# Attention and feed-forward in one stream: a new order of products, statistics taken earlier, and rstd taken for several groups at once

## The chip, the cores and the metric

One core of one Trainium2 chip. The metric is the device time of one execution in microseconds (us), as the median of several executions. Executions fall into a fast state and a slower one (some 1.7% longer, 2877 us for the kernel before); verdicts here compare fast runs with fast runs. A profiled execution of each kernel gives the trace that the views below are taken from. Engines: PE = TensorE matmul, PEld = its weight load, DVE = VectorE, ACT = ScalarE, POOL = GpSimd.

## The reference

Three residual blocks, each with a layer norm in front: causal attention over 256 time steps, banded attention over 128 bands (distance up to 16), and a feed-forward of 128 to 512 to 128 with an exact gelu. All is in fp32.

```python
B, T, FB, C = (2, 256, 128, 128); heads = 4; BAND = 16; INNER = 512
def _ln(x, w, b, eps=1e-05):
    mu = x.mean(-1, keepdims=True)
    var = ((x - mu) ** 2).mean(-1, keepdims=True)
    return (x - mu) * jax.lax.rsqrt(var + eps) * w + b
...
xt = _ln(x, ln_t_w, ln_t_b).transpose(0, 2, 1, 3)
x = x + _mha(xt, ..., causal).transpose(0, 2, 1, 3)
xf = _ln(x, ln_f_w, ln_f_b)
x = x + _mha(xf, ..., band)
xn = _ln(x, ln_n_w, ln_n_b)
h = jax.nn.gelu(xn @ w1.T + b1, approximate=False)
... # x + h @ w2.T + b2
```

The part that matters most here is the `rsqrt` of the layer norm. The kernel calls its result rstd.

## The kernel before

Work comes in groups of 512 rows (four tiles of 128). There are 128 over-time groups (`OverTime`), then 16 runs of 8 band groups (`OverBands`) and 8 feed-forward groups (`FeedForward`). PE's products go by these names: `qp`, `kp`, `vp` (queries, keys, values), `sp` (scores), `rp` (row sums of the weights), `op` (weighted values), `yp` (output of the attention), and `hp` and `zp` (the two products of the feed-forward). ACT takes the exponentials (`pt`, `pf`) and the gelu (`hT`). DVE divides `op` by `rp` (`t`, `u`, `oT`), here by way of ACT's logarithm and exponential (`ln`, `r`). A "turned block" is the normalized group transposed: it goes out to `turned` and is fetched back as `xnT`, the operand of `qp`, `kp`, `vp` and `hp`.

The loop below emits instructions in a fixed order; in step n it emits pieces of groups n-2 to n+11, and every engine takes its own instructions in that order, one after the other. This last fact carries the whole case: a POOL instruction that waits holds up every POOL instruction emitted after it.

The layer norm of one group: mean and variance on DVE (`mv`), an addition and a power on POOL (`rstd`, 128x4: one element per tile and partition), the normalization on DVE (`xh`, four instructions).

```python
    def statistics(self):
        path, vector = self.path, self.path.vector
        self.mv = path.small.tile([P, NT, 2], F32, name="mv", bufs=16)
        stats = path.small.tile([P, NT, 6], F32, name="stats")
        for i in range(NT):
            vector.bn_stats(stats[:, i, :], self.src()[:, i, :])
        for i in range(NT):
            vector.bn_aggr(self.mv[:, i, :], stats[:, i, :])

    def root(self):
        path, gpsimd = self.path, self.path.gpsimd
        self.rstd = path.small.tile([P, NT], F32, name="rstd", bufs=16)
        gpsimd.tensor_scalar(self.rstd, self.mv[:, :, 1], EPS, None, ALU.add)
        gpsimd.tensor_tensor(self.rstd, self.rstd, path.k.mhalf, ALU.pow)

    def normalize(self):
        path, vector = self.path, self.path.vector
        self.xh = path.work.tile([P, NT, P], F32, name="xh", bufs=2)
        for i in range(NT):
            vector.tensor_scalar(
                self.xh[:, i, :], self.src()[:, i, :], self.mv[:, i, 0:1], self.rstd[:, i : i + 1],
                ALU.subtract, ALU.mult,
            )
```

Attention's bias add on POOL (a 128x512 addition, called `res<-x,orow` in the over-time stage and `x<-x,orow` for the bands; the feed-forward groups have one like it, `res<-x,rows_sb`):

```python
    def bias(self):
        self.path.gpsimd.tensor_tensor(
            self.dst(), self.src(), self.path.k.orow[self.which].unsqueeze(1).to_broadcast([P, NT, P]), ALU.add
        )
```

Masks, sums and the weighted values of the over-time groups. `mask(s)` is on POOL, the first half's sum is on POOL and the second half's on DVE; PE's `rp` (row sums of the weights) needs both halves:

```python
    def first_mask(self):
        self.mask(0)
        self.add(self.path.gpsimd, 0)

    def second_half(self):
        self.scores(1)

    def second_function(self):
        self.weights(1)

    def second_mask(self):
        self.mask(1)

    def last_sum(self):
        self.add(self.path.vector, 1)

    def weigh(self):
        path = self.path
        p, v, W = self.p, self.v, self.W
        rp = path.bank([P, 2, 2 * P], "rp")
        sums = p.rearrange("p s h (n q) -> p s h n q", q=P)[:, :, :, 0:4:3, :]
        for h in range(H):
            path.tensor.matmul(rp[rows_of(h), :, :], path.k.ones[:, 0:D], sums[:, :, h], start=True, stop=True)
        op = path.bank([P, 2, 2 * P], "op")
        for s in range(2):
            for h in range(H):
                r = rows_of(h)
                path.tensor.matmul(op[r, s, :], v[:, 2 * s, r], p[:, s, h, 0 : 2 * P], start=True, stop=False)
            for h in range(H):
                r = rows_of(h)
                path.tensor.matmul(
                    op[r, s, P : 2 * P], v[:, 2 * s + 1, r], p[:, s, h, 2 * P : W], start=False, stop=True
                )
        self.op = op.rearrange("p s q -> p (s q)")
        self.rp = rp.rearrange("p s q -> p (s q)")
```

The loop. `A` is 8. `feeds[i]` and `bands[i]` tell whether group n-2+i is of that kind.

```python
        for n in range(-11, len(groups) + 2):
            feeds = [at(n - 2 + i, FeedForward) for i in range(5)]
            bands = [at(n - 2 + i, OverBands) for i in range(5)]
            do(n + 11, "load")
            do_at(n + 4, OverTime, "statistics")
            if bands[2] and feeds[1]:
                self.scalar.preload_act_table_set(EXP_SET)
            do(n, "first_half", "first_function", "first_mask")
            do_at(n + 2, Attention, "fetch")
            do_at(n + 1, FeedForward, "fetch")
            do_at(n + 2, FeedForward, "normalize", "turn")
            do_at(n + 3, Attention, "normalize", "turn")
            do_at(n + 3, FeedForward, "statistics", "root")
            do_at(n + 4, OverTime, "root")
            if bands[2]:
                do(n, "second_mask")
            do(n - 1, "weigh")
            if not feeds[1]:
                do(n - 1, "invert")
            if bands[2]:
                do(n - 2, "output", "finish")
            do(n - 1, "divide")
            do(n, "second_half", "second_function")
            if not bands[2]:
                do(n, "second_mask", "bias")
                do_at(n + A, OverBands, "bias", "statistics", "root")
            do(n + 1, "queries_keys", "take_query", "take_key")
            if not bands[2]:
                do(n - 2, "output", "finish")
            do(n + 1, "values", "take_values")
            do(n, "last_sum")
```

Of the kernel before, what the change touches and what calls it, by code (L numbers as in the profile page):

```python
# [19 lines left out]
P = 128  # L20
# [18 lines left out]
def load_constants(ctx, tc, x, t_wiT, t_woT, f_wiT, f_woT, w1T, w2T, cols, rows):  # L39
# [24 lines left out]
    k.mhalf = const.tile([P, NT], F32, name="mhalf")  # L64
# [7 lines left out]
def shifted_path(tc, k, x, out):  # L72
# [5 lines left out]
    with ExitStack() as ctx:  # L78
# [36 lines left out]
        def norm_transposed(src, w_col, b_col):  # L115
# [8 lines left out]
            nc.gpsimd.tensor_tensor(rstd, rstd, k.mhalf, ALU.pow)  # L124
# [311 lines left out]
class Group:  # L436
# [6 lines left out]
    def __init__(self, path, src, dst, before=None, store=None):  # L443
        self.path, self.src, self.dst = path, src, dst
        self.before, self.store = before, store

# [8 lines left out]
    def statistics(self):  # L455
        path, vector = self.path, self.path.vector
        self.mv = path.small.tile([P, NT, 2], F32, name="mv", bufs=16)
        stats = path.small.tile([P, NT, 6], F32, name="stats")
        for i in range(NT):
            vector.bn_stats(stats[:, i, :], self.src()[:, i, :])  # L460
        for i in range(NT):
            vector.bn_aggr(self.mv[:, i, :], stats[:, i, :])

    def root(self):
        path, gpsimd = self.path, self.path.gpsimd
        self.rstd = path.small.tile([P, NT], F32, name="rstd", bufs=16)
        gpsimd.tensor_scalar(self.rstd, self.mv[:, :, 1], EPS, None, ALU.add)
        gpsimd.tensor_tensor(self.rstd, self.rstd, path.k.mhalf, ALU.pow)

    def normalize(self):  # L470
        path, vector = self.path, self.path.vector
        self.xh = path.work.tile([P, NT, P], F32, name="xh", bufs=2)
        for i in range(NT):
            vector.tensor_scalar(
                self.xh[:, i, :], self.src()[:, i, :], self.mv[:, i, 0:1], self.rstd[:, i : i + 1],
                ALU.subtract, ALU.mult,
            )
# [70 lines left out]
class Attention(Group):  # L548
# [45 lines left out]

    def divide(self):

        path, vector = self.path, self.path.vector
        t = path.work.tile([P, NT * P], F32, name="t", bufs=2)
        vector.tensor_tensor(by_rows(t), by_tile(self.rp), by_tile(self.r0), ALU.mult)
        u = path.work.tile([P, NT * P], F32, name="u", bufs=2)  # L600
        vector.tensor_tensor(by_rows(u), by_tile(self.op), by_tile(self.r0), ALU.mult)
        self.oT = path.work.tile([P, NT * P], F32, name="oT", bufs=2)
        vector.scalar_tensor_tensor(self.oT, t, 2.0, u, ALU.subtract, ALU.mult)
# [17 lines left out]
def product(path, out, weights, x):  # L621

    for c in range(P // D):
        path.tensor.matmul(out[rows_of(c)], weights[:, rows_of(c)], x, start=True, stop=True)


class OverTime(Attention):
# [65 lines left out]

    def weigh(self):
        path = self.path
        p, v, W = self.p, self.v, self.W
        rp = path.bank([P, 2, 2 * P], "rp")
        sums = p.rearrange("p s h (n q) -> p s h n q", q=P)[:, :, :, 0:4:3, :]
        for h in range(H):
            path.tensor.matmul(rp[rows_of(h), :, :], path.k.ones[:, 0:D], sums[:, :, h], start=True, stop=True)  # L700
        op = path.bank([P, 2, 2 * P], "op")
        for s in range(2):
            for h in range(H):
                r = rows_of(h)
                path.tensor.matmul(op[r, s, :], v[:, 2 * s, r], p[:, s, h, 0 : 2 * P], start=True, stop=False)
            for h in range(H):
                r = rows_of(h)
                path.tensor.matmul(
                    op[r, s, P : 2 * P], v[:, 2 * s + 1, r], p[:, s, h, 2 * P : W], start=False, stop=True
                )  # L710
# [59 lines left out]
class FeedForward(Group):  # L770

# [20 lines left out]
    def first_half(self):  # L792
        self.hp = {}
        self.hT = self.path.work.tile([P, self.path.k.NI, NT * P], F32, name="hT")
# [41 lines left out]
class BoundedPath:  # L836
# [38 lines left out]
    def groups(self, x, out):  # L875
# [3 lines left out]
        for b in range(B):  # L879
            for f0 in range(0, FB, GA):  # L880
# [22 lines left out]
                for g in range(NT):  # L903
                    yield OverTime(self, partial(part, "x", g), partial(part, "res", g), partial(load, g), partial(store, g))
        for b in range(B):
            for r0 in range(0, T, RUN):
                run = []
                for t0 in range(r0, r0 + RUN, GB):
# [25 lines left out]
                    run += [(g, part, load, store) for g in range(NT)]  # L934
                for i, (g, part, load, _) in enumerate(run):
                    group = OverBands(self, partial(part, "x", g), partial(part, "x2", g), partial(load, g))
                    if i == len(run) - 1:
                        group.by_vector = 2
                    yield group
                for g, part, _, store in run:  # L940
                    yield FeedForward(self, partial(part, "x2", g), partial(part, "res", g), None, partial(store, g))

    def run(self, x, out):
# [17 lines left out]
        for n in range(-11, len(groups) + 2):  # L961
            feeds = [at(n - 2 + i, FeedForward) for i in range(5)]
            bands = [at(n - 2 + i, OverBands) for i in range(5)]
            do(n + 11, "load")
            do_at(n + 4, OverTime, "statistics")
            if bands[2] and feeds[1]:
                self.scalar.preload_act_table_set(EXP_SET)
            do(n, "first_half", "first_function", "first_mask")
            do_at(n + 2, Attention, "fetch")
# [3 lines left out]
            do_at(n + 3, FeedForward, "statistics", "root")  # L973
            do_at(n + 4, OverTime, "root")
# [3 lines left out]
            if not feeds[1]:  # L978
                do(n - 1, "invert")
            if bands[2]:  # L980
                do(n - 2, "output", "finish")
            do(n - 1, "divide")
            do(n, "second_half", "second_function")
            if not bands[2]:
                do(n, "second_mask", "bias")
                do_at(n + A, OverBands, "bias", "statistics", "root")
            do(n + 1, "queries_keys", "take_query", "take_key")
            if not bands[2]:
# [72 lines left out]
```

## Time and profile before

| | before |
|---|---|
| median of 3 executions | 2832.48 us (2829.37 to 2876.43) |
| span of the profiled execution | 2826.2 us, PE busy 98% |
| over-time stage (first q product to last `rp` of the stage) | 1015.3 us, 7.82 us a step |
| one run of 8 band and 8 feed-forward groups (first `hp` to the next run's) | 110.06 us: 65.07 with feed-forward, 44.98 with bands |

The last two rows are read from the timeline of PE. They are the measure used for every kernel below, since the two stages turn out to have different causes. The list of PE's waits holds almost nothing in the runs (beside the waits of the start, its only other line above 1 us is `rp` behind DVE `pt`, told in the prediction); the columns are what waited, for whom, then us in total, number of times, and the longest:

```profile
PE hp L831 <- DMA xnT<-turned: 3.0, 6, 0.9
```

One more stretch of before is needed later: POOL in the feed-forward part, in the timeline (start, duration, engine, line, operation, and in brackets the idle time before it and what ended it).

```profile
1230.01 0.23 POOL L831 TENSOR_SCALAR rstd<-mv 128x4 f32<-128x4 f32 x1 [1.40 <-DVE mv L831]
1230.33 1.04 POOL L831 TENSOR_TENSOR rstd<-rstd,mhalf 128x4 f32<-128x4 f32 x1
1231.34 1.26 POOL L831 TENSOR_TENSOR res<-x,rows_sb 128x512 f32<-128x512 f32 x1
1232.05 2.37 DVE L831 TENSOR_SCALAR xh<-x,mv,rstd 128x128 f32<-128x128 f32 x4
1232.56 1.27 POOL L831 TENSOR_TENSOR x<-x,orow 128x512 f32<-128x512 f32 x1
```

Look at what starts POOL: it waits for DVE's `mv` of this step, does a power, and then two adds. Then come the band group's addition and power, and the next wait for statistics (1.15 us, at 1236.29). So no more than two bias adds come in a row in this stretch. (`xh` for a group takes 1.11 us when no add is near and 2.37 here.)

### The profile page before, as it was taken

To read this page: it belongs to the slowest core of one execution; us is meant where nothing else is said; L and a number is where in the kernel's file an instruction comes from. 1 tells how busy PE (TensorE), PEld (TensorE's weight loads), DVE (VectorE), ACT (ScalarE), POOL (GpSimd) and SP (SyncE) were. 2 spreads that over 40 slices of the span, in tenths; PEclk is the share of its full clock that TensorE was granted. 3 is DMA by queue.
4 is the path that set the end of the run, shared out by engine and by line. 5 is a ranking of instruction groups with operands and counts; after the bars stand their busy time and mean duration, and the time that the engine had idled before them with its cause. 6 is when DMAs were issued, how large, how long until landed. Compare 5 with 4: busy or idle time off the path is not lost.

```text
span 2826.2 us, 107020 instructions
## 1 busy us (share of the span) xinstructions
PE 2757.7 (98%) x44070; PEld 1858.9 (66%) x44070; DVE 2264.5 (80%) x6462; ACT 1865.2 (66%) x3408; POOL 2057.9 (73%) x2537
## 2 busy tenths in 40 slices
PE   5999999999999989999999999999999999999998
PEld 3666666666666656766766766666667667667666
DVE  5888888888888898788787787786887877877874
ACT  2777777777777767557557566566575575675664
POOL 3999999999999996676675676676666766656762
PEclk9999999999999999999999999999999999999999
DMA  5455545454554544534434434534435445344333
GB/s 122 126 148 133 140 129 146 131 140 130 147 140 129 135 126 123 144 105 106 128 106 120 129 102 122 131 94 130 115 101 141 106 107 130 102 121 114 87 95 84
DMA packets 471313, 343.90 MB, mean 122 GB/s; under 512 B 43296, under 2 KB 405152, under 8 KB 470816
## 3 DMA queue, kind: packets, MB, share of 16 engines
q1 hardware_dynamic: 469568, 335.92, 45.6%
q8 instruction: 349, 5.72, 0.8%
q14 instruction: 148, 1.21, 0.2%
q10 hardware_dynamic: 1248, 1.05, 0.1%
HBM read 169.03 MB, written 167.77 MB: 119 GB/s over the span
## 4 chain that ended last, share of the span: by engine, by line
PE 93%; DMA 2%; POOL 2%; DVE 2%; issue 0%; SPq 0%; ACT 0%; DVEq 0%; POOLq 0%
PE zp L831 16%; PE hp L831 16%; PE sp L831 13%; PE op L831 9%; PE rp L831 9%; PE qp L831 8%; PE yp L831 7%; PE vp L831 7%; PE kp L831 7%; DMA xnT<-turned 1%; DVE xh L831 1%; POOL pf L831 1%; POOL rstd L831 1%; DMA x<-in_x 1%; POOL pt L831 1%; DMA turned<-z 0%
## 5 line engine op out<-in xcount | busy, mean ns | idle before, releaser
L831 POOL TENSOR_SCALAR_AFFINE_SELECT pf<-pf 128x512 f32<-128x512 f32 x736 | 495.4, 688 | 273.1 <-ACT pf L831 248.0
L831 ACT ACTIVATE hT<-hp,b 128x512 f32<-128x512 f32 x512 | 345.2, 687 | 479.8 <-PE hp L831 470.3
L831 DVE TENSOR_SCALAR xh<-x,mv,rstd 128x128 f32<-128x128 f32 x1536 | 621.7, 465 | 15.4 <-POOL rstd L831 15.4
L831 PEld LDWEIGHTS zp<-w2T_sb,hT 128*128 128x128 f32 x4096 | 476.9, 192 | 56.1 <-issue 51.6
L831 ACT ACTIVATE pt<-sp 128x384 f32<-128x384 f32 x1024 | 419.6, 497 | 104.6 <-PE sp L831 104.6
L831 POOL TENSOR_TENSOR rstd<-rstd,mhalf 128x4 f32<-128x4 f32 x384 | 463.5, 1207 | 32.0
L831 PE MATMUL zp<-w2T_sb,hT 128*128 128x128 f32 x4096 | 480.4, 276 | 0.1
L831 PE MATMUL hp<-xnT,w1f 128*128 128x512 f32 x1024 | 474.8, 599 | 3.3 <-DMA xnT<-turned 3.0
L831 PE MATMUL sp<-qT,kT 32*128 32x128 f32 (+1 forms) x8192 | 398.3, 317 | 0.9 <-ACT kT L831 0.8
L831 POOL TENSOR_SCALAR_AFFINE_SELECT pt<-pt 128x512 f32<-128x512 f32 x512 | 315.3, 636 | 96.6 <-ACT pt L831 96.6
L831 PEld LDWEIGHTS sp<-qT,kT 32*128 32x128 f32 x8192 | 316.5, 186 | 85.8 <-issue 31.8
L831 DVE BATCH_NORM_STATS2 stats<-x 128x6 f32<-128x128 f32 x1536 | 326.8, 273 | 7.8 <-DMA x<-in_x 7.8
L831 POOL TENSOR_SCALAR rstd<-mv 128x4 f32<-128x4 f32 x384 | 94.9, 247 | 318.3 <-DVE mv L831 318.3
L831 ACT ACTIVATE pf<-sp 128x512 f32<-128x512 f32 x512 | 264.4, 603 | 62.5 <-PE sp L831 58.5
L831 PEld LDWEIGHTS hp<-xnT,w1f 128*128 128x128 f32 x1024 | 180.9, 190 | 176.9 <-issue 103.9
L831 PE MATMUL qp<-xnT,wf 128*32 128x512 f32 x2048 | 271.5, 602 | 26.1 <-DMA xnT<-turned 26.1
L831 PEld LDWEIGHTS yp<-wn,oT 128*32 128x32 f32 x8192 | 229.1, 110 | 99.6 <-issue 51.0
L831 DVE STREAM_TRANSPOSE z<-xh 128x512 f32<-128x512 f32 x384 | 273.2, 711 | 18.8 <-DMA turned<-z 5.6
L831 PEld LDWEIGHTS vp<-wf,xnT 128*32 128x32 f32 x8192 | 232.1, 110 | 78.2 <-issue 68.6
L831 DVE TENSOR_TENSOR pf<-pf,band 128x512 f32<-128x512 f32 x144 | 127.1, 892 | 188.8 <-ACT pf L831 181.3
L831 PE MATMUL yp<-wn,oT 128*32 128x128 f32 x8192 | 271.4, 273 | 0.0
L831 PE MATMUL vp<-wf,xnT 128*32 128x128 f32 x8192 | 270.6, 273 | 0.0
(87 smaller groups left out, 4029.4 us busy)
## 6 DMA issues: line engine op xcount, KB each, us to landing
turned<-z SPq DMA_DIRECT2D x1536, 64.0 KB, 2.0
xnT<-turned SPq DMA_DIRECT2D x384, 256.0 KB, 2.7
x<-in_x SPq DMA_DIRECT2D x128, 256.0 KB, 4.7
x<-res SPq DMA_DIRECT2D x256, 128.0 KB, 3.4
x<-x SPq DMA_DIRECT2D x128, 256.0 KB, 4.2
out<-res SPq DMA_DIRECT2D x256, 128.0 KB, 2.8
w1T_sb<-in_w1T ACTq DMA_DIRECT2D x1, 256.0 KB, 3.4
w2T_sb<-in_w2T ACTq DMA_DIRECT2D x1, 256.0 KB, 3.9
```

Of the source, the lines that this page charges most:

```text
L831: return self.tc.keep_in_program_order(emit(*args, **kwargs))
```

## The change

The intent: fewer instructions on POOL (a power for four groups at once in place of four powers), less switching of PE's tiling mode, and no waiting of `rp` for DVE.

1. **op before rp** in the over-time steps: half of `op`, then `rp`, then the other half.
2. **The change from bands to feed-forward** is emitted in another order (the flag `turn` of the loop), with an exact reciprocal on DVE for the last band group in place of ACT's ln and exp.
3. **Whole products** for q, k, v in the steps beside feed-forward groups, in place of four 32-column tiles.
4. **Statistics earlier**: feed-forward four steps ahead (was three), over-time eight ahead (was four).
5. **rstd for four groups at once** (two in the feed-forward): the `mv` of the batch lie in one tile, and the addition and power are emitted with the last group of the batch.

```diff
     def statistics(self):
-        path, vector = self.path, self.path.vector
-        self.mv = path.small.tile([P, NT, 2], F32, name="mv", bufs=16)
+        path, vector, n = self.path, self.path.vector, self.together
+        if self.slot == 0:
+            self.norm["mv"] = path.small.tile([P, n * NT, 2], F32, name="mv", bufs=4)
+        self.mv = self.norm["mv"][:, self.slot * NT : (self.slot + 1) * NT]
...
     def root(self):
-        path, gpsimd = self.path, self.path.gpsimd
-        self.rstd = path.small.tile([P, NT], F32, name="rstd", bufs=16)
-        gpsimd.tensor_scalar(self.rstd, self.mv[:, :, 1], EPS, None, ALU.add)
-        gpsimd.tensor_tensor(self.rstd, self.rstd, path.k.mhalf, ALU.pow)
+
+        path, gpsimd, n = self.path, self.path.gpsimd, self.together
+        if self.slot == n - 1:
+            rstd = path.small.tile([P, n * NT], F32, name="rstd", bufs=4)
+            gpsimd.tensor_scalar(rstd, self.norm["mv"][:, :, 1], EPS, None, ALU.add)
+            gpsimd.tensor_tensor(rstd, rstd, path.k.mhalf[:, 0 : n * NT], ALU.pow)
+            self.norm["rstd"] = rstd
...
+    def invert_exactly(self):
+        self.r0 = None
+        self.r = self.path.work.tile([P, NT * P], F32, name="ln", bufs=2)
+        self.path.vector.reciprocal(self.r, self.rp)
...
 def product(path, out, weights, x):
 
+    if not path.by_columns:
+        path.tensor.matmul(out, weights, x, start=True, stop=True)
+        return
...
     def weigh(self):
         path = self.path
-        p, v, W = self.p, self.v, self.W
+        op = path.bank([P, 2, 2 * P], "op")
         rp = path.bank([P, 2, 2 * P], "rp")
-        sums = p.rearrange("p s h (n q) -> p s h n q", q=P)[:, :, :, 0:4:3, :]
+        self.weigh_one(op, 0)
+        sums = self.p.rearrange("p s h (n q) -> p s h n q", q=P)[:, :, :, 0:4:3, :]
         for h in range(H):
             path.tensor.matmul(rp[rows_of(h), :, :], path.k.ones[:, 0:D], sums[:, :, h], start=True, stop=True)
...
+        self.weigh_one(op, 1)
...
+            turn = feeds[2] and bands[1]
+            self.by_columns = at(n - 1, Attention)
             do(n + 11, "load")
-            do_at(n + 4, OverTime, "statistics")
             if bands[2] and feeds[1]:
                 self.scalar.preload_act_table_set(EXP_SET)
             do(n, "first_half", "first_function", "first_mask")
+            if turn:
+                do(n, "second_half", "second_function")
             do_at(n + 2, Attention, "fetch")
             do_at(n + 1, FeedForward, "fetch")
             do_at(n + 2, FeedForward, "normalize", "turn")
             do_at(n + 3, Attention, "normalize", "turn")
-            do_at(n + 3, FeedForward, "statistics", "root")
-            do_at(n + 4, OverTime, "root")
+            do_at(n + 4, FeedForward, "statistics", "root")
+            do_at(n + A, OverTime, "statistics", "root")
             if bands[2]:
                 do(n, "second_mask")
             do(n - 1, "weigh")
-            if not feeds[1]:
-                do(n - 1, "invert")
-            if bands[2]:
+            do(n - 1, "invert_exactly" if turn else "invert")
+            if bands[2] or turn:
                 do(n - 2, "output", "finish")
             do(n - 1, "divide")
-            do(n, "second_half", "second_function")
+            if not turn:
+                do(n, "second_half", "second_function")
             if not bands[2]:
                 do(n, "second_mask", "bias")
-                do_at(n + A, OverBands, "bias", "statistics", "root")
+                do_at(n + A, OverBands, "bias")
+                if at(n - 1, FeedForward) and at(n - 2, OverBands):
+                    do_at(n + A - 1, OverBands, "statistics", "root")
+                if not turn:
+                    do_at(n + A, OverBands, "statistics", "root")
             do(n + 1, "queries_keys", "take_query", "take_key")
-            if not bands[2]:
+            if not bands[2] and not turn:
                 do(n - 2, "output", "finish")
```

Cut: the arguments that carry a batch's tiles to its groups, `normalize` reading its slice of the batch's rstd, the last band group of a run no longer masking two heads on DVE, and two buffers for `hT`.

## The prediction

> **What bounds the kernel now.** I read the page first (engine shares, chain, groups), then busy time in stretches, then the timeline and the chain of work inside one step of each stage. The page's first part and the head of its chain:
>
> ```profile
> span 2826.2 us, 107020 instructions
> PE 2757.7 (98%) x44070; PEld 1858.9 (66%) x44070; DVE 2264.5 (80%) x6462; ACT 1865.2 (66%) x3408; POOL 2057.9 (73%) x2537
> PE 93%; DMA 2%; POOL 2%; DVE 2%; issue 0%; SPq 0%; ACT 0%; DVEq 0%; POOLq 0%
> ```
>
> PE looks full: only 68.5 us of the span are not PE (2826.2 - 2757.7). The busy table by stretches places them: about 31 in the first 42 us, 5 up to 200 us, 8 between 1000 and 1080 us, 8 at the end, a few at transfers, and some 12 in 200 to 1000 us, which is 0.12 per step of 7.82 us. The program is 128 attention-over-time steps (to about 1055 us), then 16 runs of 8 band steps (6.43 us each) and 8 feed-forward steps (7.0 us each).
>
> That 0.12 is the interesting part. One over-time step, from the timeline of 608.9 to 618.9 us:
>
> ```profile
> 616.02 0.69 DVE L831 TENSOR_TENSOR res<-yp,res 128x512 f32<-128x512 f32 x1 [0.99 <-PE yp L831]
> 616.63 1.04 DVE L831 TENSOR_TENSOR pt<-pt 128x512 f32<-128x512 f32 x1
> 616.76 0.94 PE L831 MATMUL sp<-qT,kT 32*128 32x256 f32 x16
> 617.82 1.07 PE L831 MATMUL rp<-pt,ones 128*32 128x512 f32 x8
> ```
>
> DVE's pt sum ends at 616.63 + 1.04 = 617.67 and rp starts 0.15 later. Where the list of waits does name DVE pt as rp's releaser (8 times, 10.1 us), the distance is also 0.14 to 0.15. So in every over-time step rp waits shortly on DVE, below what the list shows. The step closes as a loop: yp (PE), res and pt (DVE), rp (PE). Without that wait sp would hand over at once, as the step's second sp does (starts 612.29, the next product at 613.16, 0.87 later; the first takes 617.82 - 616.76 = 1.06). The wait costs 0.19 us a step.
>
> At the change between bands and feed-forward the chain of work shows another cost, of PE itself:
>
> ```profile
> 1436.12 1.91 PE hp L831 x4
> 1438.04 1.08 PE rp L831 x8
> 1439.12 1.15 PE op L831 x31
> 1440.27 1.91 PE hp L831 x4
> 1442.18 1.01 PE yp L831 x32
> 1443.20 1.91 PE hp L831 x4
> 1445.11 3.59 PE zp L831 x32
> 1448.70 1.72 PE hp L831 x4
> 1450.42 1.01 PE yp L831 x32
> 1451.43 1.91 PE hp L831 x4
> ```
>
> hp (whole 128x128 weights) takes 1.72 behind another whole product and 1.91 behind one in four 32-column tiles; yp 0.87 inside a column stretch and 1.01 behind a whole one. Each excursion costs about 0.33 us.
>
> **What the Trainium skill says.** (1) "TensorEngine Tiling (Array Packing)", Tiling Modes, Key Properties: changing the tiling mode drains TensorE. The trace agrees: 1.91 against 1.72. (2) "SBUF — State Buffer", "SBUF: two separate sides": VectorE and GpSimd share a port pair, locked for the whole instruction when a VectorE instruction has two SBUF inputs or runs in a two-port mode. The trace agrees: the 128x512 oT took 0.69 us, and 1.77 beside a GpSimd add at 998 us. (3) "GPSIMD Engine Reference", section 3.1: about 2.6 cycles per element for a two-input op, done in a software loop. The 128x512 add at 1.28 us fits. For the power, no page has a figure. (4) "VectorE: DVE Perf Modes", the fixed hardware budget: reciprocal is an iterative divide with a repeat count of 8. From it I estimate 512 x 8 / 0.96 GHz = 4.3 us for one 128x512; the trace before has none.
>
> **Part 1: op before rp in the over-time steps.** weigh now does half of op, then rp, then the other half. Half an op is 1.30/2 = 0.65 us, so rp is asked for 0.65 later than before, and the wait of 0.19 goes. PE's work is the same. About 122 steady steps x 0.19 = 23 us; I count 21, for weight loads behind the mode switch.
>
> **Part 2: the change to feed-forward (16 times).** Before, the ten lines above last 1453.34 - 1436.12 = 17.2 us (16.9 where op does not wait, at 1215 us). After, the order of instructions has eight hp, rp, op, yp, four hp, zp, four hp, yp whole, four hp: 3.63 + 1.08 + 0.87 + 0.87 + 1.91 + 3.59 + 1.72 + 0.89 + 1.72 = 16.3. Saved 0.6 to 0.9, say 0.8 x 16 = 13 us.
>
> **Part 3: whole q, k, v products beside feed-forward (15 times, twice each).** qp 0.99 becomes 0.86 in each: 2 x 0.13 x 15 = 4 us.
>
> **Part 4: the end of the over-time stage.** From 991 to 1056 us the chain is POOL, then DVE: the band groups' bias (1.3 us) and rstd come on top, and for four steps statistics are taken twice. PE stands idle 7.9 us there, of which about 1.3 is Part 1's wait. With one set of statistics per step everywhere and three of four powers gone: -6 us, if the power of sixteen is short.
>
> **Part 5: the start.** PE starts its first product at 41.4 us, since the first turned block went out behind sixteen loads of x and the second turned block. Now four statistics and the fifth (1.1 us each) come before the first normalization, about 2.8 us later on DVE, but the loads still fill the queue to 33.3 us, and the first fetch is issued before the second turned block. Also op no longer waits for the pt sum at 54 us. I count -3 us.
>
> **Part 6: tables and the exact reciprocal.** Table loads fall from 80 to 32 (48 x 1.28 = 62 us of ACT), all beside PE work: the feed-forward stage has ACT idle 470 us for hp. The reciprocal puts up to 4.3 us on DVE, 16 times, in place of ACT's ln and exp and one DVE product. Its oT is wanted at about 1449.8 on the scale above, and comes at about 1445 + its duration: just in time. Counted 0.
>
> **Part 7: rstd.** GpSimd's additions and powers fall from 384 each to 128 each (32 + 32 of sixteen, 64 of eight):
>
> ```profile
> L831 POOL TENSOR_TENSOR rstd<-rstd,mhalf 128x4 f32<-128x4 f32 x384 | 463.5, 1207 | 32.0
> L831 POOL TENSOR_SCALAR rstd<-mv 128x4 f32<-128x4 f32 x384 | 94.9, 247 | 318.3 <-DVE mv L831 318.3
> ```
>
> This is off PE's path, as POOL has 0.67 us idle per step, so the saving is worth nothing directly. But the longer power stands in POOL's queue between the pt sum of one half and the mask of the other, which the pt sum of DVE and then rp wait for. In the step's timeline POOL gets there at 614.1; add 0.3 for the addition, up to 0.46 for the port (the power took 1.51 there against 1.037 free), the power P, half the masks 0.62, DVE's sum 1.0, release 0.15: 616.6 + P. rp is wanted at about 618.2 with op first. A power over about 1.6 us therefore stops PE, in 30 steps.
>
> Sum without such a stop: 21 + 13 + 4 + 6 + 3 = 47 us, from a fast level of about 2831: 2784.
>
> **Rivals.** (a) The power grows with its elements. 1.037 us for four, less the 0.22 of an addition, is 0.2 per element and 3.5 for sixteen: PE stops 1.9 us, 30 times, +57 us, and Part 4 turns to nothing: about 2847. For it: GpSimd works in a software loop, and 0.8 us of overhead on a power is hard to explain. Against: an author who batches will have seen batching pay. Weight 0.4. (b) The power has a large fixed part and grows a little, 1.8 to 2.2 us: some 10 us lost, about 2795. Weight 0.25. (c) Mostly fixed, up to 1.6 us: about 2784. Weight 0.35. (d) On top, the reciprocal comes too late for yp or delays the next normalizations: 1 us x 16 = +16. (e) DVE becomes the bound of the over-time step instead (6.7 of 7.63 us busy): unlikely, it keeps 0.9 us.
>
> **Range and chances.** The median of this mixture lies near 2794. The range takes (c) with a little more at one end and (a) at the other: 2770 to 2856. Faster by 2% needs under 2776, a saving of 56 us; all parts would have to come out at their best: 0.12. Slower by 2% is over 2889: rival (a) with (d) and more: 0.03. Within 2%: 0.85.
>
> **What would show it.** Over-time steps of 7.63 us and rp not at 0.15 behind DVE pt: Part 1 right. Steps of 7.82 still: Part 1 wrong. The row of rstd 128x16 decides the rivals: 1.6 us or less for (c); about 3.5, with rp idle every fourth step behind pt, for (a). hp at 1.91 twice rather than four times per run shows Part 2; yp waiting on oT shows (d). No idle PE at 1000 us shows Part 4, a first product before 41 us Part 5. The prediction would be wrong if the wait moves to another loop of the same length, or if the first op half behind the mode switch costs what the wait cost.

## The result

The changed kernel takes **3002.57 us** (3000.20 to 3004.66, four runs) against 2830.93 us beside it. The ratio of the fast runs is 1.0608 (95% interval 1.0590 to 1.0626): slower by 6%, and outside the predicted range. Ratios in this document are the mean time of one kernel's fast runs over that of the other's of the same rounds, so not quite the ratio of the medians. The result agrees with the reference, and so did every kernel below in the comparison that is run with each.

| | before | after | difference |
|---|---|---|---|
| over-time stage | 1015.3 us | 1081.3 us | +66.0 |
| one run | 110.06 us | 116.96 us | +6.90, times 16 = +110 |
| of it feed-forward part / band part | 65.07 / 44.98 | 70.63 / 46.34 | +5.56 / +1.36 |

The two stages give 176 us; the spans of the two profiles differ by 172.2. From the page of after, the engines' busy time and the chain of work by engine:

```profile
PE 2779.0 (93%) x42534; PEld 1855.0 (62%) x42534; DVE 2432.8 (81%) x6446; ACT 1801.7 (60%) x3328; POOL 1824.4 (61%) x2057
...
PE 56%; DVE 23%; POOL 9%; DMA 6%; issue 3%; ACT 2%; SPq 1%; DVEq 0%; POOLq 0%
```

POOL has 233 us less to do than before (1824.4 against 2057.9), just as intended, and the kernel is slower. PE has nearly the same work, but the chain that ends last, which was PE to 93%, is now PE to 56% only; DVE and POOL took the rest. PE's waits say where (the views of the changed kernels name another line, since all instructions are emitted by one helper line):

```profile
PE hp L858 <- DMA xnT<-turned: 55.9, 31, 3.8
PE yp L858 <- DVE t L858: 43.8, 32, 1.5
PE rp L858 <- DVE pt L858: 41.5, 33, 1.3
```

Two of these groups (`rp`, `yp`, about 32 each) belong to the over-time stage, which has 32 batches; `hp` belongs to the runs.

With its smaller lines the list has 84 us of waits in the runs, 5.3 us a run. The rest of what the runs lose is in waits too short for the list, and a part may be the clock: the trace's clock record has eleven stretches of 3.4 us at a granted clock of 0.50 in the runs of after and none in those of before. That is 1.7 us each at most, 19 us in all; the ten runs (of fifteen) that hold one took 117.2 us on average, the five others 116.5. What brings these stretches on was not tested; a_root4 and best_mix below, which lose nothing in the runs, have none there.

The groups of instructions concerned (times are busy us, then mean ns, then the idle time before them):

```profile
L858 POOL TENSOR_TENSOR rstd<-rstd,mhalf 128x16 f32<-128x16 f32 x64 | 200.1, 3127 | 5.3
L858 POOL TENSOR_TENSOR rstd<-rstd,mhalf 128x8 f32<-128x8 f32 x64 | 111.5, 1742 | 5.3
L858 DVE TENSOR_SCALAR xh<-x,mv,rstd 128x128 f32<-128x128 f32 x1536 | 753.9, 551 | 34.9 <-POOL rstd L858 34.9
```

The power costs by its elements: undisturbed it took 1.04 us for four, 1.67 for eight and 2.93 for sixteen, which is about 0.157 us an element and 0.41 fixed. DVE's normalizations took 753.9 us in all, against 621.7 before, with the same work.

**An over-time step with a batch**, from the timeline:

```profile
612.53 3.25 POOL L858 TENSOR_TENSOR rstd<-rstd,mhalf 128x16 f32<-128x16 f32 x1
...
615.75 1.22 POOL L858 TENSOR_SCALAR_AFFINE_SELECT pt<-pt 128x512 f32<-128x512 f32 x2
616.41 1.10 DVE L858 TENSOR_TENSOR pt<-pt 128x512 f32<-128x512 f32 x1 [1.78 <-POOL pt L858]
616.94 1.71 POOL L858 TENSOR_TENSOR res<-x,orow 128x512 f32<-128x512 f32 x1
617.44 3.72 DVE L858 TENSOR_SCALAR xh<-x,mv,rstd 128x128 f32<-128x128 f32 x4
617.66 1.06 PE L858 MATMUL rp<-pt,ones 128*32 128x512 f32 x8 [1.28 <-DVE pt L858]
...
623.57 1.08 PE L858 MATMUL yp<-wn,oT 128*32 128x128 f32 x32 [1.47 <-DVE t L858]
```

Read it as two blows from one power. First: the second mask stands behind the power, DVE's sum waits 1.78 us for it, and PE's `rp` waits 1.28. Second: POOL is now late, and does its backlog without a pause (add, masks, sum); DVE's `xh` lasts 3.72 us in place of 1.10. Taken singly, its four instructions end 0.08 to 0.09 us after one of POOL's each time (at 618.74, 619.32, 619.91 and 621.16), as it would be if the two engines take turns at the port pair of the prediction's point (2). DVE's `t` and `oT` stand behind it, and `yp` waits 1.47. The four steps from 600.94 to 634.62 last 33.68 us; four steps without a stall last 30.5.

**The feed-forward part of a run**, also from the timeline of after:

```profile
1658.84 0.24 POOL L858 TENSOR_SCALAR rstd<-mv 128x8 f32<-128x8 f32 x1 [10.11 <-DVE mv L858]
1659.16 1.67 POOL L858 TENSOR_TENSOR rstd<-rstd,mhalf 128x8 f32<-128x8 f32 x1
1660.79 1.27 POOL L858 TENSOR_TENSOR res<-x,rows_sb 128x512 f32<-128x512 f32 x1
1661.90 4.00 DVE L858 TENSOR_SCALAR xh<-x,mv,rstd 128x128 f32<-128x128 f32 x4
1662.03 1.34 POOL L858 TENSOR_TENSOR x<-x,orow 128x512 f32<-128x512 f32 x1
1663.33 1.27 POOL L858 TENSOR_TENSOR res<-x,rows_sb 128x512 f32<-128x512 f32 x1
1664.55 1.26 POOL L858 TENSOR_TENSOR x<-x,orow 128x512 f32<-128x512 f32 x1
1664.89 1.96 PE L858 MATMUL hp<-xnT,w1f 128*128 128x512 f32 x4 [0.66 <-DMA xnT<-turned]
```

This is the stretch to hold against the one shown of before. POOL waited 10.11 us for the statistics of a pair, while its bias adds stood behind that wait in its queue. Then four adds came in a row, where before there were two. Counted over the whole trace from 1180 us on, before never has more than two adds in a row; after has four in a row 15 times and eight in a row 15 times, so once each in a run. `xh` lasts 4.00 us: its last three instructions take 1.30 us each, and each ends 0.08 us after one of POOL's adds. The turned block of this group is fetched later, and PE's `hp` waits for the fetch (3.8 us at worst, 31 times in all).

### The profile page after: what moved, and what is told of

Its sections match the earlier page's. It is cut to its first block, busy times and chain, and to the rows that moved or that the text cites. A ratio compares the mean times of both kernels' runs of the same rounds, so it can differ in the third digit from the quotient of the medians.

```text
span 2998.4 us, 103522 instructions
## 1 busy us (share of the span) xinstructions
PE 2779.0 (93%) x42534; PEld 1855.0 (62%) x42534; DVE 2432.8 (81%) x6446; ACT 1801.7 (60%) x3328; POOL 1824.4 (61%) x2057
## 4 chain that ended last, share of the span: by engine, by line
PE 56%; DVE 23%; POOL 9%; DMA 6%; issue 3%; ACT 2%; SPq 1%; DVEq 0%; POOLq 0%
PE zp L858 10%; DVE xh L858 9%; PE hp L858 8%; PE sp L858 8%; PE op L858 5%; PE vp L858 5%; PE qp L858 5%; PE rp L858 5%; PE kp L858 4%; PE yp L858 4%; DVE stats L858 4%; POOL rstd L858 4%; DMA xnT<-turned 4%; POOL pt L858 2%; DVE z L858 2%
## 5 line engine op out<-in xcount | busy, mean ns | idle before, releaser
L858 DVE TENSOR_SCALAR xh<-x,mv,rstd 128x128 f32<-128x128 f32 x1536 | 753.9, 551 | 34.9 <-POOL rstd L858 34.9
L858 POOL TENSOR_SCALAR_AFFINE_SELECT pf<-pf 128x512 f32<-128x512 f32 x768 | 515.5, 687 | 279.1 <-ACT pf L858 252.8
L858 POOL TENSOR_SCALAR rstd<-mv 128x16 f32<-128x16 f32 (+1 forms) x128 | 32.8, 256 | 524.8 <-DVE mv L858 524.8
L858 POOL TENSOR_TENSOR rstd<-rstd,mhalf 128x16 f32<-128x16 f32 (+1 forms) x128 | 311.6, 2435 | 10.7
L858 PEld LDWEIGHTS yp<-wn,oT 128*32 128x32 f32 (+1 forms) x7808 | 230.5, 111 | 141.5 <-DVE t L858 73.6
L858 PE MATMUL yp<-wn,oT 128*32 128x128 f32 (+1 forms) x7808 | 272.6, 273 | 45.6 <-DVE t L858 43.8
L858 PE MATMUL qp<-xnT,wf 128*32 128x512 f32 (+1 forms) x1856 | 270.6, 600 | 28.8 <-DMA xnT<-turned 28.8
L858 PEld LDWEIGHTS vp<-wf,xnT 128*32 128x32 f32 (+1 forms) x7424 | 236.4, 113 | 75.8 <-issue 65.1
L858 ACT COPY v<-vp 128x512 f32<-128x512 f32 x256 | 150.2, 587 | 210.6 <-PE vp L858 210.6
L858 PE MATMUL vp<-wf,xnT 128*32 128x128 f32 (+1 forms) x7424 | 270.9, 273 | 1.5 <-DVE t L858 1.5
```

Of the source, the lines that this page charges most:

```text
L858: return self.tc.keep_in_program_order(emit(*args, **kwargs))
```

## The experiments

Twelve kernels were run, four at a time beside the kernel before on one chip. All profiled runs were in the fast state. "Stage" is the over-time stage and "run" one run, as in the tables above.

### Undo one part of the change, or do one part alone

**a_root4**: the changed kernel with rstd per group; everything else of the change stays.

```diff
-        if self.slot == n - 1:
-            rstd = path.small.tile([P, n * NT], F32, name="rstd", bufs=4)
-            gpsimd.tensor_scalar(rstd, self.norm["mv"][:, :, 1], EPS, None, ALU.add)
-            gpsimd.tensor_tensor(rstd, rstd, path.k.mhalf[:, 0 : n * NT], ALU.pow)
+        self.rstd = path.small.tile([P, NT], F32, name="rstd", bufs=16)
+        gpsimd.tensor_scalar(self.rstd, self.mv[:, :, 1], EPS, None, ALU.add)
+        gpsimd.tensor_tensor(self.rstd, self.rstd, path.k.mhalf[:, 0:NT], ALU.pow)
```

Cut: `statistics` and `normalize`, which go back to tiles per group in the same way.

> The changed kernel, but rstd taken for each group by itself again (384 powers of 128x4); everything else of the change stays. Theory 1 (the batch is the cause everywhere: a power of sixteen takes 2.9 us and holds POOL's queue, afterwards POOL runs its adds back to back and DVE's xh is locked out): over-time steps of 7.63 us each without a slow fourth, runs of bands and feed-forward back near 109 us, total about 2800. Theory 2 (the batch costs the over-time stage only, the reordered change to feed-forward with its reciprocal of 3.33 us on DVE costs the runs): over-time stage 97 us shorter than in the changed kernel, runs still about 116 us, total about 2905.

**a_noturn**: the changed kernel with part 2 undone (`turn = False`, the old places of the bands' statistics, two heads of the last band masked on DVE).

> The changed kernel with the old order at the change to feed-forward (second half of the hidden layer after the weighing, logarithm and exponential on ACT instead of the reciprocal, two heads of the last band masked on DVE); the batch of rstd stays. Theory 1: the runs stay slow, above 114 us each, total 2980 or more. Theory 2: runs near 110 us, total about 2900, and few waits of hp for xnT.

**b_oporder**: the kernel before with part 1 alone (the new `weigh`).

> The kernel before with only the order inside weigh of the over-time steps changed: half of op, then the sums rp, then the other half. If rp's hidden wait for DVE's pt sum (0.19 us per step) is what Part 1 says: steps of 7.63 us, total about 2808 (ratio 0.992). If the wait moves elsewhere: 7.82 and 2831.

**b_turn**: the kernel before with part 2 alone (order, exact reciprocal).

> The kernel before with only the new order at the change to feed-forward (four hidden products at once, the exact reciprocal on DVE, statistics of the next bands one step later there); two heads of the last band still masked on DVE, rstd per group. My prediction's Part 2: 13 us saved, total 2818. Theory 2: runs of 114 us or more, total 2890 or more, hp waiting for xnT in the second to fifth feed-forward group.

| | median us | ratio to before (95%) | stage | run |
|---|---|---|---|---|
| a_root4 | 2800.81 | 0.990 (0.9884 to 0.9917) | 1019.3 | 108.19 |
| a_noturn | 2997.45 | 1.0601 (1.0584 to 1.0618) | 1082.5 | 116.5 |
| b_oporder | 2807.48 | 0.9927 (0.9911 to 0.9942) | 993.6 | 110.22 |
| b_turn | 2850.34 (two of four slow; the fast ones 2825.17 and 2826.90) | 0.9993 (0.9971 to 1.0014) | 1015.3 | 110.06 |

The batch is the cause in both stages: without it 202 us are gone, 62 in the over-time stage and 8.8 in each run. The rival, that the new order at the change costs the runs, fell: undoing it changed 0.5 us in a run. b_oporder confirms part 1: steps of 7.63 us, 21.7 us off the stage. b_turn gives nothing by itself. From a run's first `hp` to its second `zp` it is 0.48 us shorter (16.49 against 16.97, mean of 14 runs), 7.7 us in all; but its list of waits has `hp` waiting 8.0 us for turned blocks (3.0 before), which takes most of that back.

a_root4's stage of 1019.3 was a surprise: its steps are 7.87 us long and not 7.63, although `op` stands before `rp`. In its timeline POOL's bias add starts just ahead of DVE's sum and takes the port:

```profile
607.72 1.27 POOL L852 TENSOR_TENSOR res<-x,orow 128x512 f32<-128x512 f32 x1
607.84 1.70 DVE L852 TENSOR_TENSOR pt<-pt 128x512 f32<-128x512 f32 x1
```

In b_oporder the sum starts first (603.37, 1.10 us) and the add second (603.90, 1.71 us). The cause I supposed was the new place of the statistics, which the next run tests.

### The over-time statistics back in their place, and what is left of the batch's cost

**best_mix**: a_root4 with the over-time statistics and root at their old place and distance.

```diff
+            do_at(n + 4, OverTime, "statistics")
...
-            do_at(n + A, OverTime, "statistics", "root")
+            do_at(n + 4, OverTime, "root")
```

The first of these lines stands at the head of the step, behind `load`; a_root4's part of the edit is cut.

> The changed kernel with rstd taken per group (as in the run before that undid the batch) and, besides, the over-time groups' statistics and root put back to their place and distance of before (statistics four steps ahead at the head of the step, root after the feed-forward groups' root). The rest of the change stays. Theory M: what kept the over-time step at 7.87 us without the batch is only that place, because the power then came 0.46 us earlier and GpSimd's bias add took the port just ahead of DVE's pt sum; so the step goes to 7.63 us, the over-time stage to about 994 us (993.6 in the kernel before with only the order of op and rp changed) and the runs stay at 108.2: about 2776 us, ratio 0.981. Rival: the step's length comes from elsewhere in the change (buffers of mv and rstd, the tiling by steps), and the stage stays near 1019: about 2801 us.

**a_root4_noturn**: a_root4 with part 2 undone.

> The changed kernel with rstd per group and with the order at the change from bands to feed-forward put back as before (no exact reciprocal, the vector engine masks two heads of the last band). Against the same with the new order (2800.8 us, runs of 108.2): Theory 1: the gain of 1.9 us in each run belongs to the new order at the change, which alone did not show in the kernel before because the turned block came late; then runs of about 109.5 to 110 and 2822 to 2828 us. Theory 2: it comes from the feed-forward statistics four steps ahead, so that no step waits, and the whole products; then runs of about 108.5 and 2803 to 2807 us.

**a_paced**: the changed kernel; the addition of EPS is done for each group again, so that POOL waits for statistics in each step. The power stays batched.

```diff
+        if self.slot == 0:
+            self.norm["rstd"] = path.small.tile([P, n * NT], F32, name="rstd", bufs=4)
+        rstd = self.norm["rstd"]
+        gpsimd.tensor_scalar(rstd[:, self.slot * NT : (self.slot + 1) * NT], self.mv[:, :, 1], EPS, None, ALU.add)
         if self.slot == n - 1:
-            rstd = path.small.tile([P, n * NT], F32, name="rstd", bufs=4)
-            gpsimd.tensor_scalar(rstd, self.norm["mv"][:, :, 1], EPS, None, ALU.add)
             gpsimd.tensor_tensor(rstd, rstd, path.k.mhalf[:, 0 : n * NT], ALU.pow)
-            self.norm["rstd"] = rstd
```

> The changed kernel with the addition of EPS done per group again (one of 128x4, about 0.22 us, after each group's statistics, on GpSimd), the power still once for the batch (16 or 8 elements, unchanged durations of about 3 and 1.67 us). Theory P: in the runs the batch hurts because GpSimd no longer waits for the vector engine's statistics in every step: it waits once for two or four steps, and then sends its bias adds back to back, each of which holds up one of the vector engine's normalizations; with a wait in each step the adds come one by one again and the run goes from 117.0 to about 108.5 us, the over-time stage stays at about 1081 (there the masks pace GpSimd): about 2865 us. Theory L: the length of the powers does it; then nothing changes: about 3000 us.

**a_shortpow**: the changed kernel with the power taken of four of the batch's elements only; the others stay variances, so the result is wrong on purpose.

```diff
-            gpsimd.tensor_tensor(rstd, rstd, path.k.mhalf[:, 0 : n * NT], ALU.pow)
+            gpsimd.tensor_tensor(rstd[:, 0:NT], rstd[:, 0:NT], path.k.mhalf[:, 0:NT], ALU.pow)
```

> Wrong results on purpose: the changed kernel, batch and waits unchanged, but the power is taken of 4 of the batch's 16 or 8 elements only (1.04 us in place of 3.25, 2.93 and 1.67). Theory P: the over-time stage loses its stall of 1.3 us in each fourth step and the lockout behind it (from 1081 to about 1010 us), the runs stay at about 116 to 117 us: about 2920 us. Theory L: both recover: about 2795 us. A third view (the statistics eight steps ahead or the batch's buffers are the cause): neither recovers, about 3000 us.

| | median us | ratio to before (95%) | stage | run (feed-forward / bands) |
|---|---|---|---|---|
| best_mix | 2777.36 | 0.9818 (0.9801 to 0.9836) | 993.1 | 108.19 (64.06 / 44.13) |
| a_root4_noturn | 2795.49 | 0.9867 (0.9849 to 0.9885) | 1011.4 | 109.14 (65.01 / 44.13) |
| a_paced | 2906.01 | 1.0276 (1.0258 to 1.0295) | 1079.5 | 110.71 (64.42 / 46.29) |
| a_shortpow | 2850.13 | 1.0072 (1.0053 to 1.0090) | 993.3 | 113.14 (68.41 / 44.73) |

best_mix came out within 2 us of its expectation: the place of the statistics was what kept a_root4 at 7.87 us. It is the fastest kernel of the study, 1.8% under the kernel before.

a_paced and a_shortpow split the batch's cost. In the over-time stage the length of the power is all of it: with the short power the stage loses 88 us and is 993.3, and pacing does nothing (1079.5). (That it lands on best_mix's 993.1 is in part chance: its steady steps are 7.70 us against 7.63, and its last seven steps 57.7 us together against 63.2.) In the feed-forward part pacing is nearly all of it (70.63 to 64.42; 64.06 without a batch). In the band part pacing does nothing (46.29), so a third cost was left there. My expectation for a_paced missed it by 2 us a run, and for a_shortpow I expected no effect in the runs and saw 3.8 us a run: a shorter power also relieves them. (The comparison with the reference passed a_shortpow, although most of its rstd are wrong: rows of this input have a variance near 1.)

The third cost shows in after's own timeline, at the last but one band step:

```profile
1630.06 1.97 POOL L858 TENSOR_TENSOR rstd<-rstd,mhalf 128x8 f32<-128x8 f32 x1
...
1632.06 2.64 DVE L858 TENSOR_SCALAR xh<-x,mv,rstd 128x128 f32<-128x128 f32 x4 [1.57 <-POOL rstd L858]
...
1637.71 1.75 PE L858 MATMUL sp<-qT,kT 32*128 32x128 f32 x28 [0.75 <-DVE x L858]
```

DVE waits 1.57 us for rstd. A pair's power is emitted with its second group, so its first group has one step from the power to the normalization and not two; and in a band step POOL has four us of masks ahead of it.

a_root4_noturn must be read by its stages. Its total fits neither theory, and its six times lie at different levels: three near 2791 us, one at 2799, two near 2813, all of normal clock, and the profiled one was of the upper; a_root4 too ranges from 2794.62 to 2803.36. What tells the levels apart I did not trace. Its run, though, is 0.95 us longer than a_root4's, which was checked cleanly next.

### All three costs away with the batch kept, and the remaining parts

**a_late**: the changed kernel with the over-time root moved to the end of the step, behind the second mask and the bias add.

```diff
-            do_at(n + A, OverTime, "statistics", "root")
+            do_at(n + A, OverTime, "statistics")
...
                 do(n, "second_mask", "bias")
+                do_at(n + A, OverTime, "root")
```

> The changed kernel with the over-time root (the addition and the power of sixteen) moved in GpSimd's queue from between the two masks of a step to the end of the step, behind the second mask and the bias add. Same instructions, same durations. Theory Q: the stall of each fourth over-time step is a matter of place: between the masks the power of 3.25 us delays the second mask and with it DVE's sum and rp; behind them it delays only the next step's first mask, and GpSimd has about 2 us free in each of the steps without a root to catch up. Then the over-time stage goes from 1081 to about 1000 us (993 if nothing is left), the runs stay at 117: about 2920 us. Theory D: GpSimd is behind for a step or two wherever the power stands, and its adds then collide with the vector engine's work: the stage stays above 1050 us, 2975 us or more.

**a_rescue**: a_late, with a_paced's addition per group, and feed-forward statistics and roots five steps ahead.

```diff
-            do_at(n + 4, FeedForward, "statistics", "root")
+            do_at(n + 5, FeedForward, "statistics", "root")
```

> The batch kept, with its three costs taken away together: the addition of EPS per group again (GpSimd waits for statistics in each step), the over-time root at the end of the step, and the feed-forward statistics and roots five steps ahead in place of four (a pair's root is taken in the step of its second group, which left the first group's normalization one step after it: the vector engine waited 1.56 us for rstd in the next to last band step). If these three are the whole of the cost: runs of about 108.2 us, over-time about 1000 us, 2785 us (2775 to 2800). If the power's length costs in some other way as well, runs of 109.5 or more and over 2805 us.

**best_noturn**: best_mix with part 2 undone.

> The fastest so far (per-group rstd, over-time statistics at their old place, 2777.4 us) with the change from bands to feed-forward in its old order. The over-time stage is the same in both, so this is the clean measure of the new order. Theory 1: 0.95 us in each of 16 runs, as the two kernels with the other over-time placement showed in their stages (109.14 against 108.19): about 2792 us. Theory 2: that difference was chance or belongs to the slower of two levels which the other kernel showed: 2777 to 2782 us.

**b_op_col**: the kernel before with parts 1 and 3 (whole products).

> The kernel before with the new order of op and rp (2807.5 us alone) and, besides, whole products for q, k and v in the steps beside feed-forward groups. Theory 1: as predicted, 0.26 us in each run: 110.0 us per run, about 2803 us. Theory 2: the 0.85 us that the changed kernel without the batch gains in its band steps (44.98 to 44.13) is this part: runs of 109.3 to 109.4, about 2794 us. If neither shows, the band steps' gain comes from the feed-forward statistics being taken four steps ahead.

| | median us | ratio to before (95%) | stage | run (feed-forward / bands) |
|---|---|---|---|---|
| a_late | 2925.24 | 1.0343 (1.0313 to 1.0373) | 1008.9 | 116.78 (70.42 / 46.36) |
| a_rescue | 2792.14 | 0.9870 (0.9842 to 0.9899) | 1005.0 | 108.24 (64.12 / 44.13) |
| best_noturn | 2791.86 | 0.9869 (0.9840 to 0.9897) | 993.1 | 109.10 (64.98 / 44.12) |
| b_op_col | 2798.01 | 0.9889 (0.9860 to 0.9918) | 993.2 | 109.57 (64.69 / 44.89) |

Four of the seven runs of before beside these were slow (2877 us); the ratios use the other three.

a_late: the same instructions at another place in POOL's queue take 72 us off the over-time stage. The stall at `rp` is gone; what is left is the second blow, weaker, once a batch:

```profile
615.60 2.76 DVE L858 TENSOR_SCALAR xh<-x,mv,rstd 128x128 f32<-128x128 f32 x4
615.89 1.04 PE L858 MATMUL rp<-pt,ones 128*32 128x512 f32 x8
...
620.77 1.08 PE L858 MATMUL yp<-wn,oT 128*32 128x128 f32 x32 [0.48 <-DVE t L858]
```

`rp` has no wait in brackets any more, and `yp` waits 0.48 in place of 1.47. The list of waits has this 33 times with 15.5 us, about what is missing to best_mix's 993.

a_rescue: with all three costs away the run is 108.24 us, the same as without a batch, though the powers are as long as ever. POOL and DVE pass each other in the feed-forward part:

```profile
1213.11 1.27 POOL L859 TENSOR_TENSOR res<-x,rows_sb 128x512 f32<-128x512 f32 x1
1214.34 1.27 POOL L859 TENSOR_TENSOR x<-x,orow 128x512 f32<-128x512 f32 x1
1215.84 1.11 DVE L859 TENSOR_SCALAR xh<-x,mv,rstd 128x128 f32<-128x128 f32 x4
```

Two adds, and only then `xh`, in 1.11 us. So the account of the three costs holds together: 3002.6 us become 2792.1 (the feed-forward roots five steps ahead were not run alone). Yet best_mix, which does not batch, is 15 us faster: 12 of them are the over-time stage (1005.0 against 993.1), where `yp` still waits for DVE's `t` (13.8 us in 29 waits). In the runs the batch can be made harmless; nothing in these kernels shows it to be of use.

best_noturn against best_mix gives part 2 its clean number: 0.91 us a run, 14.5 us. b_op_col against b_oporder gives part 3: 0.65 us a run.

Not all of the 0.91 us are PE's own. The first `zp` of a run in best_noturn, with ACT before it, and then in best_mix:

```profile
1308.18 1.28 ACT L852 ACT_TABLE_LOAD   x1
1309.48 2.42 ACT L852 ACTIVATE hT<-hp,b 128x512 f32<-128x512 f32 x4
1309.65 4.31 PE L852 MATMUL zp<-w2T_sb,hT 128*128 128x128 f32 x32
...
1307.75 3.73 PE L852 MATMUL zp<-w2T_sb,hT 128*128 128x128 f32 x32
```

In the old order ACT does `ln`, `r` and three table loads of 1.28 us before these four gelus (`hT`), and `zp` goes forward only as they land. From `zp` to the next product it is 4.15 us in all fourteen runs looked at (the second to the fifteenth) of best_noturn, and 3.57 in those of best_mix. So 0.58 of the 0.91 us are a wait for ACT, in pieces too short for the list of waits, and 0.34 are PE's (the first `zp` starts 8.53 us after the run's first `hp` in best_noturn, 8.19 in best_mix). In before, the same stretch took 3.61 us on average: there the wait was still hidden.

## Why the prediction was wrong

The predicted 2794 us lay 209 us under the result. By its own steps:

**Part 1, op before rp (-21): right.** b_oporder shows steps of 7.63 us and 21.7 us off the stage. In after it was buried under the batch, and even without the batch it is lost if the statistics stand at their new place (a_root4, 7.87 us). That the wait would merely pass to a port race between POOL's bias add and DVE's sum was not among my rivals.

**Part 2, the change to feed-forward (-13): the size came out, in part by luck.** 14.5 us in best_mix; nothing in b_turn, where the turned blocks come too late. The prediction did not say that PE can only use the order if its operand is there. And of the 0.91 us a run only 0.34 come from fewer switches of PE's tiling mode, which was its reason; 0.58 come from `hT`, which no longer waits behind ACT's `ln`, `r` and table loads.

**Part 3, whole products (-4): the work was right, the time larger.** In the timelines PE needs 0.13 and 0.11 us less at the two places, 0.24 a run against the predicted 0.26. The medians differ by 9.5 us, and a run by 0.65 us. Another 0.33 us of that is the second `yp` at the change, which this edit makes whole too (from a run's first `hp` to its second `zp`: 16.65 us against 16.98); the prediction had counted that `yp` under Part 2. And `hp` waits less for turned blocks (3.3 us in all against 4.9).

**Feed-forward statistics four steps ahead: not counted, worth some 6 us.** From b_op_col to best_noturn, which differ mainly in this, the run goes from 109.57 to 109.10 us and the list of waits loses every `hp` that waits for a turned block. The band part gains 0.77 us (44.89 to 44.12); the feed-forward part gives back 0.29, as `zp`'s wait for ACT comes to light.

**Part 4, the end of the over-time stage (-6): nearly right, and outweighed.** With one set of statistics a step the four steps of 9.6 to 9.7 us near the end are gone: the stage's last seven steps take 58.1 us in a_root4 and 58.5 in after, against 63.7 before and 63.2 in best_mix, where the statistics are back at their old place. So the part is worth some 5 us. PE is not without idle time there, as the prediction had it: a_root4's steps are 8.33 us, with `rp` waiting 0.5 us for DVE. And without the batch the same place costs 27 us in 110 steady steps (7.87 against 7.63).

**Part 5, the start (-3): wrong.** The first product comes at 41.97 us in after, 41.45 before.

**Part 6, tables and reciprocal (0): right for the kernel before, too low once the turned blocks come in time.** In best_noturn, where PE no longer waits for turned blocks, the table loads, `ln` and `r` of the old order cost 0.58 us a run, some 9 us, and the new order takes them away. The reciprocal took 3.33 us where I estimated 4.3.

**Part 7, the batch (0, or +57 in rival (a)): this is the step that failed.** It failed twice.

- *Size.* Rival (a) had the power right in kind and nearly in number (3.5 us estimated, 3.25 measured in place, 2.93 free), but it got a weight of 0.4 only. The argument against it, that an author who batches will have seen batching pay, was no measurement; the trace of before had only one size, so it could tell neither way. And rival (a) took the stall to end with `rp`: 1.9 us, 30 times. Measured, the stage lost 88 us to the power's length (1081.3 against 993.3 with the short power). A batch's four steps are 3.2 us longer, since POOL's backlog then locks DVE's `xh` out and `yp` waits as well.
- *Place.* The sentence "this is off PE's path, as POOL has 0.67 us idle per step" held for POOL's busy time and missed what POOL's waits were for. In the feed-forward part POOL is idle much of the time, so I looked for no cost there at all. But the small roots were what kept POOL in step with DVE: one wait for `mv` in every step. With one wait in two or four steps the same adds came in fours and eights, and each cost DVE's normalization a gap. a_paced shows this (its adds never come more than two in a row again): an addition of 0.22 us per group, which brings back the wait, takes 6.2 us off the run's feed-forward part, 99 us in all. The band part has its own cost (2.2 us a run), a pair's power coming one step before it is needed instead of two.

Together: 88 us in the over-time stage and 8.8 us in each of 16 runs make 228 us; best_mix, which lacks just the batch and the over-time statistics' new place, is 225 us faster than after.

**Range and chances.** 0.03 for slower was far too little. All rivals were about one wait, at one place; none asked what the removed instructions had been holding back. The prediction did not see that one unmeasured duration could outweigh its sum of gains. That this sum (47 us) is near to what best_mix gains (53) is in part luck: best_mix lacks Part 4's edit, and the earlier feed-forward statistics and the wait for ACT were not in the sum.

## What to carry to other kernels

Before batching small instructions on an in-order engine, ask two things of each instruction removed: how long is the combined one, and which instruction of the queue will stand behind it; and which wait did the small ones contain, since that wait may be what spaces the work behind them. An engine that is idle half the time can still hurt another one when its work comes in bunches, if the two share a port. A test for the second is cheap: put back a tiny instruction with the old wait, and see whether the time comes back.

## What the Trainium skill lacked or had wrong

- "GPSIMD Engine Reference", section 3.1 (and no other page): there is no cost for a power. Undisturbed, a fp32 power of 128x4, 128x8 and 128x16 took 1.04, 1.67 and 2.93 us here, so 0.157 us an element and 0.41 fixed, against 1.27 us for a whole 128x512 add.
- "SBUF — State Buffer", "SBUF: two separate sides": whichever starts first is said to hold the port pair for the whole instruction. For adds the runs agree (in a row, 1.27 us each, they stretched a group's `xh` from 1.11 to 4.00 us), for the power not: in a_rescue `xh` ran in its free time of 1.11 us from 1201.69, inside a power of eight that began at 1201.32. The same holds for 63 powers of sixteen there, which had `xh` inside and took 2.93 to 2.94 us. The powers did grow where DVE's `oT`, which has two inputs in SBUF, was running when they began (32 times in a_rescue: 1.98 to 1.99 us in place of 1.67). (The recorded spans on POOL are rough.)
- "VectorE: DVE Perf Modes", the fixed hardware budget: a repeat count of 8 led me to estimate 4.3 us for a 128x512 reciprocal; 16 of them took 3.33 us on average.
